# First convolutions of two bottleneck layers on pairs of tiles, with seven half-size products in place of eight

## The chip, the cores and the metric

One core of a Trainium2 chip. The metric is device time in microseconds (us); medians of three or four runs are quoted. Executions of one kernel agree within about 0.2%. Engine names in the profile: PE is the tensor engine (PEld its weight loads), DVE is VectorE, ACT is ScalarE, POOL is GpSimd, SP is SyncE. A bank is one tile of PSUM, the memory that matmuls write and add into. A transfer's landing is the arrival of its data. Half clock is a granted TensorE clock of 0.50 in the profile.

## The reference

Two bottleneck layers in a row, in fp32, on 64 images of 1024 channels and 14 by 14 pixels:

```python
out = relu(bn(conv1x1(x, w1)))        # 1024 -> 256 channels: "first convolution"
out = relu(bn(conv3x3(out, w2)))      # 256 -> 256: "second"
out = bn(conv1x1(out, w3))            # 256 -> 1024: "third"
x   = relu(x + softplus(residual_scale) * out)
```

The batch norm takes mean and variance over the whole batch, so each convolution must be complete before it can be normalised. These are the stage boundaries. The third convolution's statistics come from a "gram" stage of its own, which multiplies the second convolution's output with itself.

## The kernel before

x lies in 32 tiles of two images (128 partitions x 8 channel blocks x 392 pixels). The first convolution is a plain product for each tile and each half of the output channels, eight matmuls into one bank:

```python
def conv1(xt, t, w1, par, stats):
    for o in range(MS):                                   # 2 output halves
        ps = psum_tile()
        for s in range(CS):                               # 8 channel blocks
            nc.tensor.matmul(ps, w1[:, s, o, :], xt[:, s, :], start=(s == 0), stop=(s == CS - 1))   # L136
        y = two(t, o)
        nc.scalar.activation(y, ps..., AF.Identity, bias=...)                                       # L138
        nc.vector.bn_stats(stats[:, o, t, :], y)                                                    # L141
```

In layer 0 ("stage one") this loop runs alone, with x from HBM. In layer 1 it is interleaved with layer 0's third convolution (L305), which makes the tiles that it needs. The 3x3 filters of both layers are transformed on VectorE during stage one. Each of four (layer, input half) pieces is loaded, six results `u` are computed one after the other into two buffers, and each is stored to HBM, from where the second convolution reads it:

```python
for s in range(MS):
    g = pool.tile(...); nc.scalar.dma_start(out=g, in_=w2s[b][:, s])
    ...                                                    # even, quad: 4 instructions
    for i in range(NF):                                    # 6
        u = pool.tile([P, NK, M], FP, tag="us")            # two buffers
        ...                                                # 3 instructions on VectorE
        nc.gpsimd.dma_start(out=us[b][i][:, s], in_=u)     # L130
...
for t in range(T):
    conv1(load_x(xpool, 0, t), t, w1, par[0], stats1)
    if t in (2, 8):
        filters(fpool, t // 8)
```

The kernel's text gives dependencies; the build orders each engine's instructions by its own estimate of when they are ready and needed, unless an instruction is pinned behind the one before it.

## Time and profile before

| | before |
|---|---|
| time | 2309.55 us (2309.44 to 2312.31) |
| TensorE busy | 97% of the span |
| first convolutions | 1024 products, 680.9 us |
| stage one ends (last product) | 349.2 us |
| boundary before the gram stage: first statistics to first normalisation | 697.70 to 705.39, 7.7 us |
| layer 1's first convolution with layer 0's third | 814.8 to 1490.5, 675.7 us |

The prediction below shows the lines and how they are read.

### The profile page before, as it was taken

To read this page: it belongs to the slowest core of one execution; us is meant where nothing else is said; L and a number is where in the kernel's file an instruction comes from. 1 tells how busy PE (TensorE), PEld (TensorE's weight loads), DVE (VectorE), ACT (ScalarE), POOL (GpSimd) and SP (SyncE) were. 2 spreads that over 40 slices of the span, in tenths; PEclk is the share of its full clock that TensorE was granted. 3 is DMA by queue.
4 is the path that set the end of the run, shared out by engine and by line. 5 is a ranking of instruction groups with operands and counts; after the bars stand their busy time and mean duration, and the time that the engine had idled before them with its cause. 6 is when DMAs were issued, how large, how long until landed. Compare 5 with 4: busy or idle time off the path is not lost. (4 is left out here: it accounts for less than half of the span.)

```text
span 2307.8 us, 22580 instructions
## 1 busy us (share of the span) xinstructions
PE 2236.0 (97%) x9264; PEld 1637.6 (71%) x9264; DVE 1077.3 (47%) x1854; ACT 581.4 (25%) x911; POOL 48.4 (2%) x102
## 2 busy tenths in 40 slices
PE   8999997999997999999999999899999899999998
PEld 4555557999997865555555555499999888555554
DVE  3431116878874333223322332377887733444443
ACT  1111115111104023223222322341111040444443
POOL 0100000000000000000000000000000000000000
PEclk9999998999998999999999999999999998999999
DMA  9864424555443033434343432245455420678774
GB/s 358 305 228 157 146 77 179 186 188 200 182 160 148 1 140 140 167 140 164 143 167 140 157 150 112 115 158 194 183 190 195 152 96 22 257 302 310 293 314 174
DMA packets 41863, 409.13 MB, mean 177 GB/s; under 512 B 4640, under 2 KB 4896, under 8 KB 7968
## 3 DMA queue, kind: packets, MB, share of 16 engines
q1 hardware_dynamic: 27936, 282.08, 33.6%
q0 software_dynamic: 12672, 118.49, 12.3%
q10 hardware_dynamic: 1152, 7.12, 0.8%
q8 instruction: 73, 1.20, 0.2%
q14 instruction: 30, 0.25, 0.0%
HBM read 289.18 MB, written 118.49 MB: 177 GB/s over the span
## 5 line engine op out<-in xcount | busy, mean ns | idle before, releaser
L136 PE MATMUL ps<-x,w 128*128 128x392 f32 x2048 | 680.9, 493 | 10.4 <-DMA w<-in_w 10.4
L305 PE MATMUL ps<-y,w 128*128 128x392 f32 x2048 | 686.2, 496 | 0.0
L136 PEld LDWEIGHTS ps<-x,w 128*128 128x128 f32 x2048 | 390.2, 191 | 295.4 <-DMA w<-in_w 10.4
L305 PEld LDWEIGHTS ps<-y,w 128*128 128x128 f32 x2048 | 392.0, 192 | 286.0 <-issue 4.4
L395 DVE SCALAR_TENSOR_TENSOR x<-ps,scale,x 128x392 f32<-128x392 f32 x512 | 320.5, 626 | 335.5 <-PE ps L305 331.7
L396 ACT ACTIVATE x<-x,shift 128x392 f32<-128x392 f32 x512 | 318.3, 622 | 380.6 <-DVE x L395 380.6
L141 DVE BATCH_NORM_STATS2 stats<-y 128x6 f32<-128x392 f32 x128 | 71.6, 567 | 497.9 <-ACT y L138 497.9
L138 ACT ACTIVATE y<-ps,par 128x392 f32<-128x392 f32 x128 | 74.2, 587 | 557.5 <-PE ps L136 516.7
L221 PE MATMUL ps<-sums,u 128*128 128x224 f32 (+1 forms) x768 | 172.1, 347 | 25.2 <-ACT t L161 12.7
L254 DVE TENSOR_TENSOR f<-ps,ms 128x448 f32<-128x448 f32 x192 | 113.4, 602 | 147.0 <-PE ps L234 79.6
L226 PE MATMUL ps<-r,u 128*128 128x224 f32 (+1 forms) x768 | 173.6, 347 | 0.0
L232 PE MATMUL ps<-r,u 128*128 128x224 f32 (+1 forms) x768 | 172.5, 346 | 0.0
L221 PEld LDWEIGHTS ps<-sums,u 128*128 128x128 f32 x768 | 137.4, 190 | 26.6 <-ACT t L161 13.3
L228 PE MATMUL ps<-r,u 128*128 128x192 f32 (+1 forms) x768 | 153.5, 321 | 0.0
L234 PE MATMUL ps<-r,u 128*128 128x192 f32 (+1 forms) x768 | 153.3, 321 | 0.0
L226 PEld LDWEIGHTS ps<-r,u 128*128 128x128 f32 x768 | 141.8, 191 | 1.3
L245 ACT ACTIVATE ms<-ps 128x448 f32<-128x448 f32 (+1 forms) x80 | 41.9, 524 | 390.5 <-PE ps L221 390.5
L232 PEld LDWEIGHTS ps<-r,u 128*128 128x128 f32 x768 | 136.3, 188 | 1.4
L228 PEld LDWEIGHTS ps<-r,u 128*128 128x128 f32 x768 | 132.5, 189 | 1.1
L234 PEld LDWEIGHTS ps<-r,u 128*128 128x128 f32 x768 | 131.9, 188 | 0.9
L336 DVE TENSOR_TENSOR zt<-ps,crow 128x512 f32<-128x512 f32 x98 | 67.8, 693 | 112.1 <-PE ps L334 112.1
L322 PE MATMUL ps<-zt 128*128 128x257 f32 x392 | 119.6, 387 | 0.5 <-DVE zt L336 0.5
(105 smaller groups left out, 1137.1 us busy)
## 6 DMA issues: line engine op xcount, KB each, us to landing
u<-u SPq DMA_DIRECT2D x96, 1280.0 KB, 5.5
x<-in_x SPq DMA_DIRECT2D x64, 1568.0 KB, 6.7
mid<-x POOLq DMA_DIRECT2D x32, 1568.0 KB, 5.4
x<-mid SPq DMA_DIRECT2D x32, 1568.0 KB, 6.6
out<-x POOLq DMA_DIRECT2D x32, 1568.0 KB, 6.3
u<-us POOLq DMA_DIRECT2D x24, 640.0 KB, 7.3
w<-in_w ACTq DMA_DIRECT2D x4, 1152.0 KB, 16.8
w<-in_w ACTq DMA_DIRECT2D x2, 1024.0 KB, 8.7
```

What stands on the lines that cost most here:

```text
L136: nc.tensor.matmul(ps, w1[:, s, o, :], xt[:, s, :], start=(s == 0), stop=(s == CS - 1))
L138: nc.scalar.activation(y, ps.rearrange("p (h l) -> p h l", h=H), AF.Identity, bias=par[:, B1 + o : B1 + o + 1])
L221: nc.tensor.matmul(m[:, o, :n], w(s, D1D2), sums[:, s].rearrange("p l c -> p (l c)"), start=(s == 0), stop=(s == MS - 1),)
L226: nc.tensor.matmul(odd, w(s, D1), r[:, s, :, WH:], start=(s == 0), stop=False)
L228: nc.tensor.matmul(odd[:, :, : WH - 1], w(s, D3), r[:, s, :, WH + 1 :], start=False, stop=(s == MS - 1))
L232: nc.tensor.matmul(even, w(s, D2), r[:, s, :, :WH], start=(s == 0), stop=False)
L234: nc.tensor.matmul(even[:, :, 1:], w(s, D0), r[:, s, :, : WH - 1], start=False, stop=(s == MS - 1))
L254: nc.vector.tensor_tensor(f[:, o].rearrange("p r (i q c) -> p q (r i) c", i=GI, q=2)[:, :, :lines], eos[o][:, :, :n].rearrange("p q (l c) ...
L305: nc.tensor.matmul(ps.rearrange("p (h l) -> p h l", h=H), w3[:, s, o, :], two(t, s), start=(s == 0), stop=(s == MS - 1))
L322: nc.tensor.matmul(g0, zt[:, c, 0:P], zt[:, c, :], start=first, stop=last)
L395: nc.vector.scalar_tensor_tensor(v, ps, scale[:, o : o + 1], v, ALU.mult, ALU.add)
L396: nc.scalar.activation(v, v, AF.Relu, bias=shift[:, o : o + 1])
```

## The change

Intent: a pair of tiles is a product of 2 by 2 blocks (two output halves, two halves of the input channels, two tiles). With Winograd's form of Strassen's method it takes seven half-size products in place of eight, for some sums of inputs, weights and results. A half product is four matmuls. The core of the diff, cut where marked:

```diff
+    def load_w1(pool, b):            # four transfers in place of one
+        w = pool.tile([P, MS, 2, CS // 2, P], FP, tag="w1", ...)
+        for o in range(MS):
+            for h in range(2):
+                nc.scalar.dma_start(out=w[:, o, h], in_=w1s[b][:, o, h])
+    def combine_w1(pool, b, w):      # four sums of weights on VectorE (L113 to L116)
+        nc.vector.tensor_add(s[:, 0], a[1][0], a[1][1])
+        ...
+    def matmul(*args, **kw):         # first and third convolutions: pinned order
+        tc.keep_in_program_order(nc.tensor.matmul(*args, **kw))
     def filters(b):
-            g = pool.tile(...)       # and even, quad, us
+            spare = y_all[:, s, NPX // 2 - GPX :]        # scratch: tail of y from tile 12 on
+            g, even, quad = ...; u = part(15 * M + (i % 2) * NK * M, NK, M)   # two u per input half
-            nc.scalar.dma_start(out=g, in_=w2s[b][:, s])
+            nc.sync.dma_start(out=g, in_=w2s[b][:, s])
+    class Conv1:
+        p1: bu  = A11 X11;  u1 = copy(bu)            (ScalarE)
+        p2: bx  = A12 X21;  y11 = bx + u1            (VectorE)
+        t1: v1 = X12 - X11                           (VectorE, 128 x 1568; L215)
+        t23: v3 = X22 - X12 (L219); v2 = v3 + X11 (L220)
+        p6: bu += S2 v2;    u2 = copy(bu);  v2 = X21 - v2   (L229)
+        p7: bu += S3 v3;    u3 = copy(bu)
+        p5: bp  = S1 v1;    c22: y22 = bp + u3       (VectorE, L198)
+        p4: bu += A22 v2;   y21 = bu
+        p3: bp += S4 X22;   y12 = bp + u2
...
-        for t in range(T):
-            conv1(load_x(xpool, 0, t), t, w1, par[0], stats1)
-            if t in (2, 8):
-                filters(fpool, t // 8)
+        w1 = combine_w1(one, 0, w1)
+        now = start(0); now.p1()
+        for t in range(0, T, 2):
+            now.t23(); now.t1(); now.p2(); now.p6()
+            if t + 2 < T: after = start(t + 2); after.p1()
+            now.p7(); now.p5(); now.c22(); now.p4(); now.p3()
+            now = after
+            if t in (0, 6):
+                filters(t // 6)
...  (layer 1: the same class between the parts of residual(); x buffers 5 -> 4; PSUM pools per stage;
...   w1 = combine_w1(one, b + 1, w1) stands after the third convolution's scale in the text)
```

The class is written here as its formulas (A are the four blocks of w1, S1 to S4 their sums, X the four blocks of the pair).

More of the change, by code (lines that the diff above doesn't have):

```diff
@@ L55 @@
 LINE = GI * W
+BANKS = dict(bu=2, bx=1, bp=1)
 BUFS = dict(u=3, t=3, r=4, sums=4, ms=3, f=2)
@@ L73, in bottlenecks @@
     small = ctx.enter_context(tc.tile_pool(name="small", bufs=2))
-    psum = ctx.enter_context(tc.tile_pool(name="psum", bufs=8, space=bass.MemoryType.PSUM))
     dram = ctx.enter_context(tc.tile_pool(name="dram", bufs=1, space=bass.MemoryType.DRAM))
@@ L87, in two, with psum_pool, load_x @@
         return y_grp[:, s, t // (GI // G), :, j * G * W : (j + 1) * G * W]
-    def load_x(pool, b, t):
+    def psum_pool(bufs=8):
+        return tc.tile_pool(name="psum", bufs=bufs, space=bass.MemoryType.PSUM)
+    def load_x(pool, b, t, parts=1):
         xt = pool.tile([P, CS, PX], FP, tag="x", name=f"x_{b}_{t}")
-        nc.sync.dma_start(out=xt.rearrange("p s f -> p (s f)"), in_=x[t] if b == 0 else mids[t])
+        n = CS // parts
+        for i in range(parts):
+            nc.sync.dma_start(
+                out=xt[:, i * n : (i + 1) * n, :].rearrange("p s f -> p (s f)"),
+                in_=(x[t] if b == 0 else mids[t])[:, i * n * PX : (i + 1) * n * PX],
+            )
         return xt
     def load_w1(pool, b):
-        w = pool.tile([P, CS, MS, P], FP, tag="w1", name=f"w1_{b}")
-        nc.scalar.dma_start(out=w, in_=w1s[b])
-        return w
+        w = pool.tile([P, MS, 2, CS // 2, P], FP, tag="w1", name=f"w1_{b}")
+        for o in range(MS):
+            for h in range(2):
+                nc.scalar.dma_start(out=w[:, o, h], in_=w1s[b][:, o, h])
+        return w
+    def combine_w1(pool, b, w):
+        a = [[w[:, o, h] for h in range(2)] for o in range(MS)]
+        s = pool.tile([P, 4, CS // 2, P], FP, tag="w1s", name=f"w1s_{b}")
+        nc.vector.tensor_add(s[:, 0], a[1][0], a[1][1])
+        nc.vector.tensor_sub(s[:, 1], s[:, 0], a[0][0])
+        nc.vector.tensor_sub(s[:, 2], a[0][0], a[1][0])
+        nc.vector.tensor_sub(s[:, 3], a[0][1], s[:, 1])
+        return a, [s[:, i] for i in range(4)]
     def load_w3(pool, b):
@@ L102, in load_w3, with psum_tile, filters, part @@
         return w
-    def psum_tile(n=PX):
+    def matmul(*args, **kw):
+        tc.keep_in_program_order(nc.tensor.matmul(*args, **kw))
+    def psum_tile(psum, n=PX):
         return psum.tile([P, 512], FP, tag="ps", name="ps")[:, :n]
-    def filters(pool, b):
+    def filters(b):
         for s in range(MS):
-            g = pool.tile([P, 3, 3 * M], FP, tag="w2", name=f"w2_{b}_{s}")
-            nc.scalar.dma_start(out=g, in_=w2s[b][:, s])
-            even = pool.tile([P, 3 * M], FP, tag="even", name="even")
-            quad = pool.tile([P, 3 * M], FP, tag="quad", name="fquad")
+            spare = y_all[:, s, NPX // 2 - GPX :]
+            def part(first, n, m):
+                return spare[:, first : first + n * m].rearrange("p (n m) -> p n m", n=n)
+            g = part(0, 3, 3 * M)
+            even, quad = part(9 * M, 2, 3 * M)[:, 0], part(9 * M, 2, 3 * M)[:, 1]
+            nc.sync.dma_start(out=g, in_=w2s[b][:, s])
             nc.vector.tensor_add(even, g[:, 0], g[:, 2])
@@ L118, in filters @@
             for i in range(NF):
-                u = pool.tile([P, NK, M], FP, tag="us", name="us")
+                u = part(15 * M + (i % 2) * NK * M, NK, M)
                 r = u[:, 0:3, :].rearrange("p k m -> p (k m)")
@@ L130, in filters, with __init__, product, bank @@
                 nc.gpsimd.dma_start(out=us[b][i][:, s], in_=u)
-    def conv1(xt, t, w1, par, stats):
-        for o in range(MS):
-            ps = psum_tile()
-            for s in range(CS):
-                nc.tensor.matmul(ps, w1[:, s, o, :], xt[:, s, :], start=(s == 0), stop=(s == CS - 1))
-            y = two(t, o)
-            nc.scalar.activation(
-                y, ps.rearrange("p (h l) -> p h l", h=H), AF.Identity, bias=par[:, B1 + o : B1 + o + 1]
-            )
-            nc.vector.bn_stats(stats[:, o, t, :], y)
+    class Conv1:
+        def __init__(self, psum, pool, pair, ts, w1, par, stats):
+            self.psum, self.pool, self.ts, self.par, self.stats = psum, pool, ts, par, stats
+            (self.a, self.s), (self.xa, self.xb) = w1, pair
+            self.half = [[t[:, h * CS // 2 : (h + 1) * CS // 2, :] for t in pair] for h in range(2)]
+        def product(self, bank, w, b, first, last):
+            n = CS // 2
+            for i in range(n):
+                matmul(
+                    bank, w[:, i, :], b[:, i, :], start=first and i == 0, stop=last and i == n - 1,
+                    skip_group_check=True,
+                )
+        def bank(self, tag):
+            return self.psum.tile([P, 512], FP, tag=tag, name=tag, bufs=BANKS.get(tag, 1))[:, :PX]
+        def t(self, tag):
+            return self.pool.tile([P, CS // 2, PX], FP, tag=tag, name=tag, bufs=1)
+        def keep(self, bank, tag):
+            v = self.pool.tile([P, PX], FP, tag=tag, name=tag, bufs=1)
+            nc.scalar.activation(v, bank, AF.Copy)
+            return v
+        def result(self, o, i, bank, more=None):
+            t, bias = self.ts[i], self.par[:, B1 + o : B1 + o + 1]
+            y, ps = two(t, o), bank.rearrange("p (h l) -> p h l", h=H)
+            if more is None:
+                nc.scalar.activation(y, ps, AF.Identity, bias=bias)
+            else:
+                nc.vector.scalar_tensor_tensor(
+                    y, ps, bias, more.rearrange("p (h l) -> p h l", h=H), ALU.add, ALU.add
+                )
+            nc.vector.bn_stats(self.stats[:, o, t, :], y)
+        def p1(self):
+            self.bu = self.bank("bu")
+            self.product(self.bu, self.a[0][0], self.half[0][0], True, True)
+            self.u1 = self.keep(self.bu, "u1")
+        def p2(self):
+            b = self.bank("bx")
+            self.product(b, self.a[0][1], self.half[1][0], True, True)
+            self.result(0, 0, b, self.u1)
+        def t1(self):
+            self.v1 = self.t("t1")
+            nc.vector.tensor_sub(self.v1, self.half[0][1], self.half[0][0])
+        def t23(self):
+            self.v3, self.v2 = self.t("t3"), self.t("t2")
+            nc.vector.tensor_sub(self.v3, self.half[1][1], self.half[0][1])
+            nc.vector.tensor_add(self.v2, self.v3, self.half[0][0])
+        def p5(self):
+            self.bp = self.bank("bp")
+            self.product(self.bp, self.s[0], self.v1, True, True)
+        def p6(self):
+            self.product(self.bu, self.s[1], self.v2, False, True)
+            self.u2 = self.keep(self.bu, "u2")
+            nc.vector.tensor_sub(self.v2, self.half[1][0], self.v2)
+        def p7(self):
+            self.product(self.bu, self.s[2], self.v3, False, True)
+            self.u3 = self.keep(self.bu, "u3")
+        def c22(self):
+            self.result(1, 1, self.bp, self.u3)
+        def p4(self):
+            self.product(self.bu, self.a[1][1], self.v2, False, True)
+            self.result(1, 0, self.bu)
+        def p3(self):
+            self.product(self.bp, self.s[3], self.half[1][1], False, True)
+            self.result(0, 1, self.bp, self.u2)
@@ L147, in norm, with conv2 @@
             nc.scalar.activation(y, y, AF.Relu, bias=shift[:, s : s + 1], scale=scale[:, s : s + 1])
-    def conv2(pool, b, par, aff, stats):
+    def conv2(psum, pool, b, par, aff, stats):
         pairs = [(g, p) for g in range(NG) for p in ((1, 2), (3, 4), (0, NF - 1))]
@@ L210, in products @@
                 n = lines * WH
-                m = psum_tile(2 * RT * GI * WH).rearrange("p (o n) -> p o n", o=MS)
+                m = psum_tile(psum, 2 * RT * GI * WH).rearrange("p (o n) -> p o n", o=MS)
                 eos = []
@@ L215, in w @@
                         return u[:, s, k, o * P : (o + 1) * P]
-                    eo = psum_tile(2 * RT * GI * WH).rearrange("p (q n) -> p q n", q=2)
+                    eo = psum_tile(psum, 2 * RT * GI * WH).rearrange("p (q n) -> p q n", q=2)
                     odd, even = (eo[:, q, :n].rearrange("p (l c) -> p l c", c=WH) for q in range(2))
@@ L300, in conv2, with conv3 @@
             acc = finish(g, pair, products(now), acc)
-    def conv3(t, o, w3):
-        ps = psum_tile()
+    def conv3(psum, t, o, w3):
+        ps = psum_tile(psum)
         for s in range(MS):
-            nc.tensor.matmul(
+            matmul(
                 ps.rearrange("p (h l) -> p h l", h=H), w3[:, s, o, :], two(t, s), start=(s == 0), stop=(s == MS - 1)
@@ L308, in conv3, with gram @@
         return ps
-    def gram(pool, aff, crow):
-        g0, g1 = psum_tile(M + 1), psum_tile(P + 1)
+    def gram(psum, pool, aff, crow):
+        g0, g1 = psum_tile(psum, M + 1), psum_tile(psum, P + 1)
         zts = [pool.tile([P, CH, M + 1], FP, tag=f"zt{i}", name=f"zt{i}") for i in range(NZT)]
@@ L329, in gram @@
                 normed += 1
-            tp = psum_tile(CH * M)
+            tp = psum_tile(psum, CH * M)
             for c in range(CH):
@@ L344, in gram, with conv3_stats @@
         return g0, g1
-    def conv3_stats(pool, grams, w3, ccol, mv):
+    def conv3_stats(psum, pool, grams, w3, ccol, mv):
         g0p, g1p = grams
@@ L359, in conv3_stats @@
             nc.vector.tensor_add(m[:, s, 0:1], d, ccol[:, s : s + 1])
-        quad = psum_tile(3 * CS).rearrange("p (o k) -> p o k", k=3)
+        quad = psum_tile(psum, 3 * CS).rearrange("p (o k) -> p o k", k=3)
         ones = keep.tile([P, 1], FP, tag="ones", name="ones")
@@ L366, in conv3_stats @@
             cols = slice(h * half, (h + 1) * half)
-            t0, t1 = psum_tile(half * P), psum_tile(half * P)
+            t0, t1 = psum_tile(psum, half * P), psum_tile(psum, half * P)
             nc.tensor.matmul(t0, g0[:, 0:P], w3[:, 0, cols, :], start=True, stop=True)
@@ L386, in conv3_stats, with residual @@
         nc.vector.tensor_sub(mv[:, :, 1], r[:, :, 2], sq)
-    def residual(pool, b, t, w3, aff):
+    def residual(psum, pool, b, t, w3, aff):
         scale, shift = aff
         xt = load_x(pool, b, t)
+        yield xt
         for o in range(CS):
-            ps = conv3(t, o, w3)
+            ps = conv3(psum, t, o, w3)
             v = xt[:, o, :]
@@ L396, in residual @@
             nc.scalar.activation(v, v, AF.Relu, bias=shift[:, o : o + 1])
-        to = mids[t] if b == 0 else out[t]
-        nc.gpsimd.dma_start(out=to, in_=xt.rearrange("p s f -> p (s f)"))
-        return xt
+            if o == CS - 1:
+                to = mids[t] if b == 0 else out[t]
+                nc.gpsimd.dma_start(out=to, in_=xt.rearrange("p s f -> p (s f)"))
+            yield xt
     def stats_tile(n, name):
@@ L467, in bottlenecks @@
     stats1 = stats_tile(MS, "stats1_0")
-    with tc.tile_pool(name="first", bufs=1) as one, tc.tile_pool(name="first_x", bufs=4) as xpool, tc.tile_pool(
-        name="filters", bufs=2
-    ) as fpool:
+    with tc.tile_pool(name="first", bufs=1) as one, tc.tile_pool(
+        name="first_x", bufs=4
+    ) as xpool, psum_pool() as psum:
         w1 = load_w1(one, 0)
+        pair = [load_x(xpool, 0, t, 2) for t in range(2)]
         for b in range(2):
@@ L476, in bottlenecks, with start @@
         masks.make_identity(nc, ident)
-        for t in range(T):
-            conv1(load_x(xpool, 0, t), t, w1, par[0], stats1)
-            if t in (2, 8):
-                filters(fpool, t // 8)
+        def start(t):
+            xs = pair if t == 0 else [load_x(xpool, 0, t + i) for i in range(2)]
+            return Conv1(psum, one, xs, (t, t + 1), w1, par[0], stats1)
+        w1 = combine_w1(one, 0, w1)
+        now = start(0)
+        now.p1()
+        for t in range(0, T, 2):
+            now.t23()
+            now.t1()
+            now.p2()
+            now.p6()
+            after = None
+            if t + 2 < T:
+                after = start(t + 2)
+                after.p1()
+            now.p7()
+            now.p5()
+            now.c22()
+            now.p4()
+            now.p3()
+            now = after
+            if t in (0, 6):
+                filters(t // 6)
     for b in range(2):
@@ L490, in bottlenecks @@
         stats2 = stats_tile(MS, f"stats2_{b}")
-        with tc.tile_pool(name=f"conv2_{b}", bufs=1) as pool:
-            conv2(pool, b, pb, aff, stats2)
-        with tc.tile_pool(name=f"last_{b}", bufs=1) as one, tc.tile_pool(name=f"last_x_{b}", bufs=5) as xpool:
+        with tc.tile_pool(name=f"conv2_{b}", bufs=1) as pool, psum_pool() as psum:
+            conv2(psum, pool, b, pb, aff, stats2)
+        with tc.tile_pool(name=f"last_{b}", bufs=1) as one, tc.tile_pool(
+            name=f"last_x_{b}", bufs=4 if b == 0 else 5
+        ) as xpool:
             w3 = load_w3(one, b)
@@ L498, in bottlenecks @@
             aff = affine(aggregate(stats2, MS), MS, pb, G2, BE2)
-            grams = gram(one, aff, crow)
-            mv3 = small.tile([P, CS, nc.vector.BN_AGGR_DIM], FP, tag="mv3", name="mv3")
-            conv3_stats(xpool, grams, w3, ccol, mv3)
+            with psum_pool() as psum:
+                with tc.tile_pool(name=f"gram_{b}", bufs=1) as pool:
+                    grams = gram(psum, pool, aff, crow)
+                mv3 = small.tile([P, CS, nc.vector.BN_AGGR_DIM], FP, tag="mv3", name="mv3")
+                conv3_stats(psum, xpool, grams, w3, ccol, mv3)
             aff = affine(mv3, CS, pb, G3, BE3, conv_bias=B3)
@@ L505, in bottlenecks, with run @@
             if b == 1:
-                for t in range(T):
-                    residual(xpool, b, t, w3, aff)
+                with psum_pool() as psum:
+                    for t in range(T):
+                        for _ in residual(psum, xpool, b, t, w3, aff):
+                            pass
                 return
             stats1 = stats_tile(MS, f"stats1_{b + 1}")
-            ahead = residual(xpool, b, 0, w3, aff)
-            for t in range(T):
-                xt, ahead = ahead, residual(xpool, b, t + 1, w3, aff) if t + 1 < T else None
-                conv1(xt, t, w1, par[b + 1], stats1)
+            w1 = combine_w1(one, b + 1, w1)
+            def run(steps, n=None):
+                while n != 0 and next(steps, None) is not None:
+                    n = n and n - 1
+            with psum_pool(4) as psum, tc.tile_pool(name=f"conv1_{b + 1}", bufs=1) as pool:
+                before, rest = None, residual(psum, xpool, b, 0, w3, aff)
+                for t in range(0, T, 2):
+                    xa = next(rest) if t == 0 else xn
+                    run(rest)
+                    if before is not None:
+                        before.p4()
+                        before.p3()
+                    rest = residual(psum, xpool, b, t + 1, w3, aff)
+                    xb = next(rest)
+                    now = Conv1(psum, pool, (xa, xb), (t, t + 1), w1, par[b + 1], stats1)
+                    run(rest, CS // 2)
+                    now.t1()
+                    run(rest)
+                    now.p1()
+                    now.p2()
+                    now.p5()
+                    now.t23()
+                    now.p6()
+                    if t + 2 < T:
+                        rest = residual(psum, xpool, b, t + 2, w3, aff)
+                        xn = next(rest)
+                        run(rest, 1)
+                    now.p7()
+                    now.c22()
+                    before = now
+                before.p4()
+                before.p3()
 def kernel(**inputs):
@@ L530, in packed @@
         w1 = get("w1").reshape(P, MS, P, CS).transpose(2, 3, 1, 0)
+        w1 = w1.reshape(P, 2, CS // 2, MS, P).transpose(0, 3, 1, 2, 4)
         w2 = get("w2").reshape(P, MS, P, MS, 3, 3).transpose(2, 3, 4, 5, 1, 0).reshape(P, MS, 3, 3 * M)
```

## The prediction

> **What bounds the kernel now.** I read the page's busy shares first, then the costliest groups, then who waited for whom on the tensor engine, then busy time by stage.
>
> ```profile
> PE 2236.0 (97%) x9264; PEld 1637.6 (71%) x9264; DVE 1077.3 (47%) x1854; ACT 581.4 (25%) x911; POOL 48.4 (2%) x102
> ...
> L136 PE MATMUL ps<-x,w 128*128 128x392 f32 x2048 | 680.9, 493 | 10.4 <-DMA w<-in_w 10.4
> L305 PE MATMUL ps<-y,w 128*128 128x392 f32 x2048 | 686.2, 496 | 0.0
> ```
>
> TensorE is busy for 97% of the span, and the first convolutions (L136) take 680.9 us of it. Each fp32 product has two records, so 2048 records are 1024 products: 680.9/1024 = 0.665 us each. The column's mean of 493 ns overlaps its neighbour and is not the pitch. The busy share alone would not prove a full engine, since ends are modelled; the waits do.
>
> ```profile
> PE ps L334 <- ACT y L147: 23.6, 4, 11.0
> PE ps L221 <- ACT t L161: 12.7, 1, 12.7
> PE ps L221 <- DVE sums L201: 12.5, 1, 12.5
> PE ps L136 <- DMA w<-in_w: 10.4, 1, 10.4
> ```
>
> Columns: total us, times, longest. The waits sit at four stage boundaries and at the start; inside a convolution there are none. So removed matmul time should come off one for one, unless a new wait appears. By stage (us, then busy us of PE, PEld, DVE, ACT, POOL, clock, DMA share, GB/s):
>
> ```profile
> 10.40:349.20 338.80, 338.77 (x1024) 195.40 (x1024) 83.60 (x178) 37.87 (x68) 13.34 (x24) 1.00 0.57 207
> 806.00:1491.00 685.00, 684.52 (x2084) 398.11 (x2084) 199.59 (x338) 196.69 (x321) 17.01 (x32) 0.99 0.36 141
> 0.00:57.70 57.70, 47.31 (x140) 27.29 (x141) 20.16 (x61) 6.24 (x12) 4.76 (x13) 1.00 0.93 358
> 57.70:115.40 57.70, 57.70 (x177) 33.38 (x176) 24.57 (x47) 7.08 (x13) 5.86 (x12) 1.00 0.85 305
> ```
>
> The first row is layer 0's first convolution, the second is layer 1's, which is interleaved with layer 0's third. VectorE is used for 25% and 29% there: room for the new additions on average. The last two rows are the filter preparation in the first stage, where DMA is at 93% and 85%. There VectorE waits for filter buffers (start, us, engine, line, what, idle before):
>
> ```profile
> 46.25 0.42 DVE L129 TENSOR_TENSOR us<-us 128x256 f32<-128x256 f32 x1
> 55.54 0.56 DVE L122 TENSOR_SCALAR us<-w 128x768 f32<-128x768 f32 x1 [8.87 <-DMA u<-us]
> ...
> 140.57 5.71 DVE L141 BATCH_NORM_STATS2 stats<-y 128x6 f32<-128x392 f32 x12
> ```
>
> A filter instruction held VectorE's queue for 8.87 us, and twelve statistics instructions piled up behind such waits until 140.57. It cost nothing, because no matmul needed those statistics. After the change matmuls will need VectorE.
>
> **What the Trainium skill says.** "VectorE: DVE Perf Modes", section "Why `tensor_tensor` can't do 2×_2P or 4×": a sum of two tensors needs both read ports, so fp32 gets one result per cycle. The trace agrees: 448 elements take 0.620 us and 896 take 1.084, a slope of (1.084-0.620)/448 = 1.036 ns per element. "TensorE: Matmul & The Clock Gate", section "Architectural detail: the array is 16× 32×32, not 1× 128×128": VectorE and ScalarE are strict FIFO; the pile of twelve above agrees. Same page, section "The HAM clock gate (the "warmup" mystery)": after about 3.4 us of idleness the matmul clock falls to half. Here the first four matmuls after a wait of 12.68 us took 1.83 us, where later groups of four take 0.92; so a long new gap costs about 2 us more than its length and a short one doesn't. "PSUM — Partial Sum Buffer", section "The four PSUM rules": a matmul without the start flag adds to what the bank holds, and a partial sum may be read in the middle. The new chain of sums depends on it; no run shows it yet, because before every bank is finished before it is read.
>
> **The change, part by part.** A convolution of a pair of x tiles is a 2 by 2 block product (two output halves, two input-channel halves, two tiles), done with seven half products in place of eight. A half product is 4 matmuls.
>
> 1. *Matmuls removed.* A pair falls from 32 products to 28. In stage one: 338.77/512 = 0.662 us each, 64 fewer, 42.3 us. In layer 1: 21.06 us per 32 products (in order of time, one tile's start at 1448.22 and the next work's at 1458.76, 10.54 us per 16), 0.659 us each, 64 fewer, 42.1 us. Together 84.4 us.
>
> 2. *VectorE added.* Per pair four sums of 128x1568: 1.084 + 672 x 0.001036 = 1.78 us each, 7.1 us (an estimate from the slope). Three results are added from PSUM by VectorE at 0.63 us (the row of L395 has that form), 1.9 us; four statistics at 0.57 us stay, 2.3 us. In all 11.3 us of a pair's 28 x 0.66 = 18.5 us. In layer 1 there are 16 residual additions besides, 10.0 us: 21.3 of 21.1 + 18.5 = 39.6 us. It fits both, so it lies beside the matmuls. ScalarE gets three copies of about 0.59 us (duration of L138) and loses three results: no change.
>
> 3. *New waits in steady state.* Three sums share a bank: a product must wait until the sum before it has been copied out, about 0.2 us to see the end plus 0.59 plus a signal, 0.9 us. In stage one a half product of the next pair (2.63 us) lies between, or P5 does; in layer 1 one third-convolution output (1.32 us) does. Both cover 0.9. The tightest: P3 adds to P5's bank, which VectorE must have read during P4's 2.63 us; it needs 0.2 + 0.63 + 0.1 and may find a 1.78 us sum ahead of it, 2.7 us, so up to 0.1 lost. The second-factor sum of the next pair can start only when P4 has read the buffer, and is needed 5.26 us later. Nothing lost. Layer 1's last pair lacks the filler: 0.9 twice, 2 us. Stage one's last pair, 1 us.
>
> 4. *Start.* The first half product needs only a quarter of w1 and half of x0, so it starts earlier than 10.4 us. But the third product needs both tiles, 3.2 MB plus 1 MB of weights and parameters: at 321 GB/s in the first 10.4 us (busy time by stage) and up to 430 after it (the view of the DMA queues), about 13 us, then two sums of 1.78 us, so 17 us. Two products of 2.63 us are done by then: the effective start is 17 - 5.3 = 11.7, and the gap is long enough for a half clock again, 2 us. Loss 3 us.
>
> 5. *Filters in y's spare part.* The same 24 filter tiles, but both input halves have buffers of their own and may overlap. By pitch of the rows, VectorE needs about 11.1 us for each of four halves, 44 us. They must be gone by the time the seventh pair writes there. Six pairs are 6 x 18.5 = 111 us after a start at 12; the demand is 44 + 6 x 11.3 = 112 us. So VectorE is nearly full for six pairs, and its queue holds waits of up to 9 us on DMA landings, while slack before a matmul starves is 2 to 5 us. I take 8 us lost, an allowance between none (everything interleaves) and 25 (each of a dozen waits costs two).
>
> 6. *Pinned order, four x buffers in layer 1, w1 in four transfers.* An x load takes 6.6 us to land and its buffer comes free a pair (39 us) ahead: nothing. The stage before third convolution had them filling PSUM during 3.2 us of scale computation (814.76 to 817.95); four banks hold 5.3 us, so nothing is lost.
>
> Sum: 84.4 - 2 - 1 - 3 - 8 = 70.4, so 2309.55 - 70.4 = 2239 us, a factor of 1.031.
>
> **The rivals.** (a) *VectorE becomes the bound while filters are made.* For it: term 5's balance without reserve and waits in a strict queue. Against: the transfers' DMA share in stage one is 0.57 on average, and filter work is pieces of at most 0.96 us. It would cost 15 to 30 us: 2246 to 2261. (b) *Short waits in every pair*, from the shared banks and the pinned order, since no other matmul may fill a gap. One us per pair is 32 us: 2263. Against: each chain of term 3 has a filler. (c) *Everything overlaps*, also the start: 84.4 less 3, 2228. (d) *Loads bound stage one.* A pair needs 3.2 MB in 18.5 us, 174 GB/s, and once the filters are done (150 to 340 us) the stage ran at a DMA share of 0.38; so not beyond the first 100 us.
>
> **Range and chances.** Best case (c) with a little more at the start gives 2226; (a) in full gives 2260. Range 2226 to 2260. Two per cent is 46 us, or 2263; that takes (a) and (b) at once, or a layer 1 that doesn't gain. Faster by over 2%: 0.89; within: 0.10; slower: 0.01.
>
> **What would show it.** Matmul records at stage-one shape fall from 2048 to 1792, with unchanged pitch; layer 1's stage shortens by 40 us without waits inside; stage one by some 30, with its lost time in the first 130 us as waits of PE on VectorE sums and of VectorE on filter landings. After the seventh pair a pair takes 18.5 us. Wrong would be: a regular wait in each pair (rival b), a stage boundary grown by more than 3 us, or waits on x loads in layer 1.

## The result, and the profile after

2289.6 us (2287.83 to 2290.83, four runs) against 2310.39 for before in the same rounds: ratio 0.9908, 95% interval 0.9891 to 0.9926. A ratio is the mean time of one kernel's runs over that of the other's runs in the same rounds, so it is not quite the ratio of the medians. The output is correct. The change gained 21 us where 70 were predicted, which lies outside the range; the prediction had given 0.89 to more than 2% faster, and this is within 2%.

First the page of the changed kernel: busy shares and the groups that answer to L136 and L305 (all pinned matmuls now have the helper's line L126, so the tiles tell them apart).

```profile
PE 2164.1 (95%) x9008; PEld 1592.5 (70%) x9008; DVE 1357.5 (59%) x2086; ACT 571.0 (25%) x911; POOL 48.3 (2%) x102
...
L126 PE MATMUL ps<-y,w 128*128 128x392 f32 x2048 | 686.7, 495 | 0.6 <-DVE quad L485 0.3
...
L126 PE MATMUL bu<-t,w1s 128*128 128x392 f32 x512 | 187.1, 510 | 29.4 <-DVE t L220 28.1
```

The engine has 9264 - 9008 = 256 records fewer, as predicted. But its busy share fell too: the time is in new idleness, named in the last column. Who the tensor engine waited for (total us, times, longest):

```profile
PE ps L437 <- ACT y L250: 39.1, 4, 26.4
PE bu L126 <- DVE t L220: 28.1, 3, 12.2
PE bp L126 <- DVE y L198: 7.4, 2, 5.7
PE bu L126 <- DMA w<-in_w: 7.0, 1, 7.0
PE bu L126 <- ACT u L189: 1.9, 3, 0.6
```

Two things grew: waits inside stage one for VectorE's sums (L220, L198), and the wait at the gram stage (before: 23.6 in total, 11.0 the longest; now 39.1 and 26.4). By stretch, in the columns that the prediction explains:

```profile
7.04:150.00 142.96, 107.49 (x284) 59.76 (x285) 105.28 (x173) 12.76 (x26) 13.17 (x24) 0.86 0.77 288
150.00:352.60 202.60, 201.93 (x613) 116.01 (x611) 117.81 (x121) 23.64 (x44) 0.00 (x0) 1.00 0.42 151
703.00:727.00 24.00, 0.14 (x1) 0.17 (x2) 8.40 (x22) 2.18 (x3) 0.00 (x0) 0.53 0.73 287
833.40:1469.60 636.20, 634.80 (x1920) 365.49 (x1920) 336.39 (x450) 189.79 (x321) 17.00 (x32) 1.00 0.40 154
```

| | before | after | predicted after |
|---|---|---|---|
| stage one ends | 349.2 | 352.6 | 319 |
| boundary before the gram stage | 7.7 | 23.1 (701.89 to 725.02) | 7.7 |
| layer 1's stretch | 675.7 | 636.1 (833.46 to 1469.6) | 635.6 |

Layer 1 gained its 40 us to within a microsecond. Stage one gained nothing: after 150 us it runs nearly without a wait (201.93 of 202.60 us busy), but before that the tensor engine was busy for only 107.49 of 142.96 us. And one boundary, where no matmul was changed, lost 15 us.

The boundary, in order of time (start, us, engine, line, what, in brackets the idle time before and its releaser), first its two ends in the kernel before, then the changed kernel:

```profile
697.70 3.84 DVE L289 BATCH_NORM_STATS2 stats<-y 128x6 f32<-128x392 f32 x8
...
705.39 20.72 ACT L147 ACTIVATE y<-y,shift,scale 128x1568 f32<-128x1568 f32 x13 [1.61 <-DVE shift L435]
```

```profile
705.65 1.89 DVE L512 BATCH_NORM_AGGREGATE mv<-stats 128x2 f32<-128x192 f32 x2
717.84 0.69 DVE L115 TENSOR_TENSOR w1s<-w 128x512 f32<-128x512 f32 x1 [10.31 <-DMA w<-in_w]
718.45 0.16 DVE L523 TENSOR_SCALAR v<-mv 128x2 f32<-128x2 f32 x1
...
721.79 0.69 DVE L113 TENSOR_TENSOR w1s<-w 128x512 f32<-128x512 f32 x1 [3.10 <-DMA w<-in_w]
...
725.02 20.72 ACT L250 ACTIVATE y<-y,shift,scale 128x1568 f32<-128x1568 f32 x13 [6.17 <-DVE shift L540]
```

The scale of the second convolution (L523 and on) was ready to be computed at 707.5. In VectorE's queue the build had put sums of layer 1's weights ahead of it and between it. They are first needed about 140 us later (861.90), but they waited for w1 to land, 10.31 and 3.10 us, and everything behind them waited too.

Stage one, the first and the last of its bad places, tensor engine and VectorE:

```profile
41.50 2.80 PE L126 MATMUL bx<-x,w 128*128 128x392 f32 x8
56.51 5.59 PE L126 MATMUL bu<-t,w1s 128*128 128x392 f32 x8 [12.21 <-DVE t L220]
```

```profile
47.39 0.95 DVE L156 SCALAR_TENSOR_TENSOR y<-y 128x768 f32<-128x768 f32 x1
48.26 1.79 DVE L219 TENSOR_TENSOR t<-x 128x1568 f32<-128x1568 f32 x1
50.44 0.96 DVE L156 SCALAR_TENSOR_TENSOR y<-y 128x768 f32<-128x768 f32 x1 [0.39 <-DMA u<-y]
...
54.67 1.79 DVE L220 TENSOR_TENSOR t<-t,x 128x1568 f32<-128x1568 f32 x1
...
126.11 0.96 DVE L156 SCALAR_TENSOR_TENSOR y<-y 128x768 f32<-128x768 f32 x1 [6.42 <-DMA u<-y]
...
131.35 1.78 DVE L220 TENSOR_TENSOR t<-t,x 128x1568 f32<-128x1568 f32 x1
```

At 41 to 56 us VectorE is busy nearly without a gap: filter work (the rows of y<-y) stands in front of and between the two sums, and the product that needs L220 starts 12.21 us late. From 119.7 to 131 us it is mostly idle, yet the sum comes late too: a filter instruction at the head of the queue waits 6.42 us for a store to land and free its buffer. The half clock after such a wait costs more: the product after the wait of 12.21 us took 5.59 us in place of 2.80.

So there are two candidates within stage one, work in front and waits for landings, both by way of the strict queue. The rivals: the sheer volume of VectorE work, and late transfers.

### The profile page after: what moved, and what is told of

Same layout as the page of the kernel before. It is cut to its first block, busy times and chain, and to the rows that moved or that the text cites. A ratio compares the mean times of both kernels' runs of the same rounds, so it can differ in the third digit from the quotient of the medians.

```text
span 2286.1 us, 22406 instructions
## 1 busy us (share of the span) xinstructions
PE 2164.1 (95%) x9008; PEld 1592.5 (70%) x9008; DVE 1357.5 (59%) x2086; ACT 571.0 (25%) x911; POOL 48.3 (2%) x102
## 4 chain that ended last, share of the span: by engine, by line
PE 90%; issue 4%; DVE 2%; DMA 2%; ACT 1%; POOL 0%; ACTq 0%; POOLq 0%
PE ps L126 29%; PE bu L126 14%; PE bp L126 7%; PE ps L329 6%; PE ps L324 6%; PE ps L335 6%; PE ps L331 5%; PE ps L337 5%; PE ps L425 4%; PE bx L126 3%; PE ps L426 2%; PE ps L437 2%; DMA w<-in_w 1%; DMA u<-y 1%; PE ps L483 1%
## 5 line engine op out<-in xcount | busy, mean ns | idle before, releaser
L126 PE MATMUL ps<-y,w 128*128 128x392 f32 x2048 | 686.7, 495 | 0.6 <-DVE quad L485 0.3
L126 PEld LDWEIGHTS ps<-y,w 128*128 128x128 f32 x2048 | 391.1, 191 | 287.7 <-issue 4.4
L126 PE MATMUL bu<-t,w1s 128*128 128x392 f32 x512 | 187.1, 510 | 29.4 <-DVE t L220 28.1
L126 PEld LDWEIGHTS bu<-t,w1s 128*128 128x128 f32 x512 | 100.1, 197 | 105.5 <-DVE t L220 21.4
L189 ACT ACTIVATE u<-bu 128x392 f32<-128x392 f32 x96 | 47.7, 497 | 385.2 <-PE bu L126 385.2
L229 DVE TENSOR_TENSOR t<-x,t 128x1568 f32<-128x1568 f32 x32 | 57.3, 1792 | 84.2 <-PE bu L126 84.2
```

The costliest lines, as they stand in the source:

```text
L126: tc.keep_in_program_order(nc.tensor.matmul(*args, **kw))
L229: nc.vector.tensor_sub(self.v2, self.half[1][0], self.v2)
```

## The experiments

Ten kernels, each timed in three rounds beside the kernel before, whose median was 2310.4 to 2310.9 us every time, so times of different sessions are compared directly. "Changed" is the kernel of the diff; times are medians.

**1. Layer 1's weight sums behind the scale** (changed, with one pin):

```diff
-        nc.vector.tensor_add(s[:, 0], a[1][0], a[1][1])        # and the three after it
+        pin(nc.vector.tensor_add(s[:, 0], a[1][0], a[1][1]))
-            w1 = combine_w1(one, b + 1, w1)
+            w1 = combine_w1(one, b + 1, w1, tc.keep_in_program_order)
```

> Only change: layer 1's four weight sums are kept behind the scale computation on VectorE. Theory A (strict queue): the changed kernel's wait before the gram stage grew by 15.4 us (from 7.7 us between first statistics of the second convolution and the first normalisation to 23.1 us) because these sums stood in VectorE's queue, waiting 10.3 and 3.1 us for w1, ahead of the scale. Then the gap falls back to about 7.7 us and the time by 15 us, to about 2274 us; first stage unchanged. Rival (w1 and x transfers themselves, or the four issues on ScalarE's queue, delay the stage): under 3 us gained, and the wait reappears elsewhere.

Measured: 2274.48 us, ratio to before 0.9844, correct. That is 15.1 us less than the changed kernel, and the gap is 7.7 us again:

```profile
702.43 3.84 DVE L392 BATCH_NORM_STATS2 stats<-y 128x6 f32<-128x392 f32 x8
...
710.13 25.47 ACT L250 ACTIVATE y<-y,shift,scale 128x1568 f32<-128x1568 f32 x16 [1.61 <-DVE shift L540]
```

The w1 transfers are as they were; only what stood behind them in the queue was set free. The boundary is settled.

**2. Filter transfers without filter arithmetic** (changed; wrong result):

```diff
-            nc.vector.tensor_add(even, g[:, 0], g[:, 2])       # and all filter arithmetic
             for i in range(NF):
-                nc.gpsimd.dma_start(out=us[b][i][:, s], in_=u)
+                nc.gpsimd.dma_start(out=us[b][i][:, s], in_=part(0, NK, M))
```

> Filter transfers as before (four loads, 24 stores of the same size) but without any filter arithmetic on VectorE; result wrong on purpose. Theory A (VectorE's queue holds the convolution's sums up behind filter work): the four waits of the first stage after its start (12.2, 5.7, 1.7, 7.9 us and the half clock after them, about 35 us in all) vanish, the first stage ends near 318 us in place of 352.6, time about 2254 us. Rival (transfers: x or the shared DMA engines are late): at least half of the waits stay, time above 2270 us.

Measured: 2260.14 us, 29.5 less than the changed kernel; 35 had been expected. Three of the four waits are gone. One stayed, and it is of another kind:

```profile
78.86 1.79 DVE L204 TENSOR_TENSOR t<-x 128x1568 f32<-128x1568 f32 x1 [13.28 <-DMA x<-in_x]
80.57 0.62 DVE L183 SCALAR_TENSOR_TENSOR y<-bp,par,u 128x392 f32<-128x392 f32 x1
...
81.24 5.60 PE L126 MATMUL bp<-x,w1s 128*128 128x392 f32 x8 [6.96 <-DVE y L183]
```

A sum of the next pair waited for its x at the head of the queue, with a result behind it that could have run. That x tile was late by this experiment's own doing: stores now read the filter tile itself, so the second layer's load of it waits for them, and the x loads stand behind that load in SyncE's queue. In the changed kernel neither VectorE nor the tensor engine ever waits for x after the start of stage one, so late x explains none of its waits; but the mechanism is the same.

**3. Filter arithmetic and transfers, without the landing waits** (changed; wrong result):

```diff
-                nc.gpsimd.dma_start(out=us[b][i][:, s], in_=u)
+                nc.gpsimd.dma_start(out=us[b][i][:, s], in_=part(0, NK, M))
```

> Filter arithmetic and transfers both stay, but the stores read another place, so no filter instruction waits for a store to land; result wrong on purpose; the scheduler may order VectorE anew. Theory A1 (waits for landings inside the queue are the larger part): the waits of 5.7, 1.7 and 7.9 us go, the one of 12.2 (VectorE busy without a gap) stays: about 20 us gained, 2270 us. Rival V (sheer volume of VectorE work): the waits stay about as large in sum, under 8 us gained.

Measured: 2270.55 us, 19 less, which is the expected number, but partly by luck. The three waits went, as expected. One wait is left in stage one after the start:

```profile
61.69 4.29 PE L126 MATMUL bu<-t,w1s 128*128 128x392 f32 x8 [18.15 <-DVE t L220]
```

But the wait of 12.2 us, which was to stay, grew to 18.15: the build, free of the buffers, put still more filter work ahead of the second pair's sums. The order changed with the dependency, so this run doesn't separate the two candidates cleanly. The next ones fix the order.

**4. Filter work spread over nine pairs, VectorE's order pinned** (changed, with run 1's pin). All VectorE instructions of stage one are pinned; the filter work becomes 32 parts, one or two in each of three gaps of a pair; the two input halves take turns; scratch is moved to the last 19 x 256 columns of y, so that it may be used until the tenth pair; `even` and `quad` get tiles of their own. The core of the edit, without the conditions for the first parts:

```diff
+            now.p2(); some(k, 1); now.c11()
+            now.p6(); some(k, 1); now.t2b()
+            ...; after.p1(); now.p7(); some(k, 2); after.t3()
+            now.p5(); now.c22(); after.t1(); now.p4m(); after.t2(); now.c21(); now.p3m(); now.c12()
-            nc.sync.dma_start(out=g, in_=w2s[b][:, s])
+            nc.gpsimd.dma_start(out=gs[s], in_=w2s[b][:, s])
```

> Right result. The same filter arithmetic, stores and buffer count, but all VectorE work of the first stage in a fixed order with the filter work cut in 32 pieces and given to gaps of nine pairs (filters placed later in y), two rows of the filters alternating so that a buffer comes round once per pair; plus the late weight sums of the first run. Theory A (order and waits in the queue, not volume): no wait over 2 us in the first stage after its start, stage ends at 318 to 323 us, and with the 15 us of the boundary about 2242 us. Rival V (volume): VectorE can't hold it and the first stage still loses over 15 us, time above 2258 us.

Measured: 2249.06 us, ratio 0.9733, correct. After its start stage one has no wait above 1 us, with the same arithmetic and stores, so their volume by itself is no bound. (Over nine pairs, that is; whether six would hold it isn't tested. The changed kernel doesn't suggest that VectorE was full there: it was busy for 105.28 of the 142.96 us before 150 us.) The missing 7 us are in the start, where one thing went wrong:

```profile
35.29 5.56 PE L126 MATMUL bu<-t,w1s 128*128 128x392 f32 x8 [19.79 <-DVE t L242]
```

My filter loads were issued at 1.3 us on GpSimd's queue, ahead of half of what the start needs.

**5. The same with the filter loads on SyncE's queue, behind the first x loads:**

```diff
-            nc.gpsimd.dma_start(out=gs[s], in_=w2s[b][:, s])
+            nc.sync.dma_start(out=gs[s], in_=w2s[b][:, s])
```

> The spread kernel again, but its four filter loads go through SyncE's queue behind the first x loads, as in the changed kernel. The spread kernel's only wait in the first stage (19.8 us before the first third product) came with its filter loads issued at 1.3 us on GpSimd's queue, w1 landing at 18 to 21 us and the parameters at 25 to 29 us. Theory A (start lost to these loads): the third product starts at 20 to 23 us in place of 35.3, 12 to 15 us gained, about 2236 us, no other wait over 2 us. Rival (the fixed VectorE order itself delays the start): start stays above 30 us, time above 2245 us.

Measured: 2233.92 us, ratio 0.9666 (0.9651 to 0.9680), correct. The third product starts at 20.39 us in place of 35.29, and this stretch of the stage has neither waits nor a lower clock:

```profile
60.00:140.00 80.00, 80.00 (x244) 46.17 (x243) 67.91 (x88) 9.31 (x18) 5.84 (x11) 1.00 0.81 298
```

VectorE is 85% busy there and DMA 81%, and the tensor engine never waits. So the order itself doesn't delay the start, and the loads did. In the changed kernel the same 80 us held 64.70 us of tensor work and 59.07 of VectorE work.

**6. A changed start on top of it:** softplus moved to the eleventh pair, and the first pair's fifth product, which needs half of x1, ahead of its sixth.

```diff
+        now.p1(); now.p2(); some(0, 1); now.t1(); now.p5(); now.t3(); now.t2()
+            if t == 20:
+                sps = [softplus(p, b) for b, p in enumerate(par)]
```

> The kernel of the run before plus a changed start: the softplus chain moved to the eleventh pair and the first pair's fifth product (needs only half of x1) put ahead of its sixth. Theory: the start is bound by the landing of x1 and then two sums of 1.79 us; one product of 2.63 us moves into that wait and the sums stand behind no parameter: 3 to 6 us less than the run before, about 2232 us. Rival (landing alone decides): under 2 us.

Measured: 2232.33 us, ratio 0.9661, correct: 1.6 us less than run 5, and the intervals of the two overlap. Both beat the changed kernel and the one before. The expectation of 3 to 6 us was missed: the sixth product moved up only to 19.19 us with one more product done before it, and then the next pair's first product met its own x still in flight:

```profile
24.74 4.59 PE L126 MATMUL bu<-x,w 128*128 128x392 f32 x8 [2.68 <-DMA x<-in_x]
```

**7. Run 5 with the filter work of each layer in one piece:**

```diff
-            some(k, 1); ... some(k, 1); ... some(k, 2)      # in each pair's gaps
+            if t in (0, 12):
+                some(k, 16)
```

> As the run with later loads, same instructions and buffers, VectorE order fixed, but the filter work of each layer stands in one piece of 16 parts (about 22 us of VectorE work plus waits for landings) between two pairs. Theory A (what stands ahead of the convolution's sums in the strict queue decides): two waits of 15 to 25 us each in the first stage, time 2268 to 2290 us. Rival V (volume of VectorE work decides, place doesn't): time within 5 us of that run.

Measured: 2270.11 us, 36 more than run 5. VectorE had no wait for a landing at all in this run; the two blocks of filter work, each 24 us long, were enough:

```profile
PE bu L126 <- DVE t L253: 30.8, 2, 15.4
```

Each block costs 15.4 us of waiting and a product at half clock (5.53 and 5.57 us). Work in front of the sums is shown as a cause by itself.

**8. One sum moved in the changed kernel's first pair**, so that the two sums that the sixth product needs come ahead of the one for the fifth:

```diff
-            now.t1()
+            now.t1(tc.keep_in_program_order if t == 0 else lambda ins: ins)
```

> The changed kernel with one sum moved: in the first pair the sum for the fifth product comes after the two sums that the sixth needs (in the changed kernel it ran first, 16.32 to 18.1 us). If that order cost the start, the wait of 7.96 us falls by 1.8 us and the time to about 2288; if the landing of x1's second half (about 18.5 us) decides, nothing changes (2289.6).

Measured: 2286.05 us, 3.5 less than the changed kernel, but the intervals of the two ratios overlap (0.9878 to 0.9907, and 0.9891 to 0.9926). What is shown is the start, by one trace of each. The third product in the changed kernel, then in this one:

```profile
22.73 5.57 PE L126 MATMUL bu<-t,w1s 128*128 128x392 f32 x8 [7.96 <-DVE t L220]
```

```profile
20.79 5.18 PE L126 MATMUL bu<-t,w1s 128*128 128x392 f32 x8 [5.86 <-DVE t L220]
```

The order cost the start 2 us, as the first theory said. The rest of the gain I don't ascribe, since this kernel's own times (2283.89 to 2288.28) scatter by more.

**9. Run 5 with the halves one after the other**, so that a buffer comes round after two parts:

```diff
-        for i in range(NF):
-            for s in range(MS):
+        for s in range(MS):
+            for i in range(NF):
```

> The kernel of the run with later loads, same instructions, buffers and slots in the fixed VectorE order, but the filters' two input halves are worked one after the other (as in the changed kernel's text) in place of by turns, so a filter buffer comes round after two parts in place of four, 5 to 10 us in place of 18; a store takes 7 us to land (median). Theory A1 (a filter instruction that waits for a landing holds up the convolution's sums behind it): VectorE waits for landings appear in the first stage, 2 to 5 us each, part of them starve the tensor engine, 5 to 20 us slower than that run (2239 to 2254 us). Rival (slack absorbs the landings; only the amount of work in front counts): within 3 us of it.

Measured: 2234.42 us, no different from run 5. I had expected waits of 2 to 5 us; there were four, and the longest was 1.9 us. A miss of size, and a useful one: waits that short cost nothing here.

**10. The same with one buffer per half:**

```diff
-                u = bufs[s][i % 2]
+                u = bufs[s][0]
```

> The kernel of the run before (halves in turn) with one filter buffer per half in place of two, so each part waits for the part before it to land (6.1 us median there); same amount of VectorE work and same order. That run's waits of at most 1.9 us cost nothing. Theory A1 (a wait for a landing at the head of the strict queue starves the tensor engine once it is longer than the slack of 1.4 to 6 us): waits of 3 to 7 us in each of eight pairs, 15 to 45 us slower, 2249 to 2279 us, the tensor engine waiting on VectorE sums or results. Rival (only work in front counts, waits for landings don't): within 3 us of 2234.

Measured: 2283.53 us, 49 more than run 9, a little beyond the expected range. Who waited for whom in it, VectorE first:

```profile
DVE y L166 <- DMA u<-y: 46.5, 12, 5.8
DVE y L163 <- DMA u<-y: 12.5, 3, 4.6
```

```profile
PE bp L126 <- DVE y L210: 39.6, 6, 9.6
```

Arithmetic and order are those of run 9. Fifteen waits for landings of up to 5.8 us (59 us in sum) turned into 40 us of waiting on the tensor engine, and half clock after it. Before the wait of 9.6 us at 64.08, for instance, two waits for landings (2.33 and 4.51 us) stood ahead of one result. So waits for landings are shown as a cause by themselves as well, once they exceed what the pair can absorb.

## Why the prediction was wrong, point by point

- *Matmuls removed* (84.4 us). Right: 256 records fewer, and an undisturbed half product starts 2.633 us after the one before, so 128 x 0.658 = 84.3 us. (In what follows a loss is the spacing of the starts of products less 2.633.)
- *VectorE's cost and steady waits* (parts 2 and 3). Right: the sums took 1.785 to 1.792 us on average (1.78 estimated), and in layer 1 and after 150 us in stage one no bank or buffer holds a product up. The last pairs waited three times 0.6 us and lost 2.7 us in all; 3 had been taken. The correct output is the first run of this case that shows partial sums read in the middle of a sum.
- *Start* (3 us). Wrong in size: 8.5. The third product started at 22.73 us, not 17, so the effective start is 17.5 us, 7.1 later than before; the half clock after the wait cost 3.0, not 2, and 1.5 comes off because the kernel before began at half clock too. Before that product VectorE ran the softplus chain until 16.3 us and then a sum that wasn't urgent. From run 8, 2 us of it is order. The landing was taken too early as well: in run 6, with the softplus moved away, the sum that needs all of x1 still waited for x until 15.43 us, where the prediction had 13.
- *Filters* ("I take 8 us lost"). This is the main step that failed: the size put on an overlap that wasn't there. The four waits are 12.2 + 5.7 + 1.7 + 7.9 = 27.5 us by the profile and 28.2 by spacing, and the half clock after them 8.0, so 36. The prediction had the parts: a strict queue, waits of up to 9 us at its head, VectorE nearly full until the scratch is overwritten. It then took an even interleaving and a small allowance. But the order in the queue is set at build time, before any landing is known (and it isn't the text's order, which has each layer's filter work in one block between two pairs): it put more than 10 us of filter work ahead of sums that a product was due to need, and waits for landings ahead of others. Rival (a) placed the loss rightly, in VectorE's queue while filters are made, though what held the sums up was order and waits rather than a full engine. The upper end of its range, 30 us, was nearly the size; it was treated as the unlikely case.
- *Volume.* The balance "44 + 6 x 11.3 = 112 of 111 us" was sound arithmetic, but it isn't what cost the time: run 5 does the same work over nine pairs beside the matmuls without a wait, and in the changed kernel VectorE was busy for 74% of the stretch before 150 us. Whether six pairs could hold it is untested.
- *w1 in four transfers, buffers, pools: "nothing"* (part 6). Wrong: 15.4 us, the second step that failed. One of the prediction's own signs of being wrong, a boundary grown by more than 3 us, came true here. I looked at what x, PSUM and transfers would do and not at the four new weight sums, which part 2 doesn't list either; they had no urgency and could stand anywhere in VectorE's queue. Run 1 shows that their place alone made the loss.
- *Layer 1* (40.1 us gained net). Right: 39.6.

Together: -84.3 + 8.5 + 36 + 2.7 + 15.4 = -21.7, and the two profiled runs differ by 21.7 (2309.54 and 2287.83 us). With order repaired (run 5) the kernel takes 2233.9 us; the prediction without its 8 us for the filters gives 2231. So its matmul arithmetic held, and what failed was the assumption about where VectorE's work would stand. What stays open is how the 36 us divide between work in front and landings in the changed kernel itself: runs 7 and 10 show both causes, each in an order of my own. The changed kernel's trace suggests work in front for the wait of 12.2 us, and landings for those of 5.7 and 7.9 (VectorE stood 5.09 and 6.42 us for a store just before them), but no run tests that division alone.

## What to carry to other kernels

When an engine with slack joins the critical path, its busy share says little: ask what stands ahead of each urgent instruction in its strict queue, and what the head of that queue may wait for. Pin urgent instructions, cut other work on that engine into pieces smaller than the slack, and give its buffers a round trip longer than a transfer takes to land. Preparatory work for a later stage wants a pin too, since the build may place it in front of a stage boundary, as in run 1's boundary here.

## What the Trainium skill lacked or had wrong

- "TensorE: Matmul & The Clock Gate", section "Architectural detail: the array is 16× 32×32, not 1× 128×128", says that VectorE is strict FIFO, but neither there nor in the pages I read is it said what a blocked head costs when a build orders the queue: here four small weight sums cost 15.1 us (run 1), waits of up to 1.9 us cost nothing (run 9), and waits of up to 5.8 us cost 49 us (run 10).
- The same page, section "The HAM clock gate (the "warmup" mystery)", gives an idle window of about 3.4 us before the half clock. After waits of 5.68, 7.91 and 12.21 us the trace agrees (products of 5.12 to 5.59 us in place of 2.80), but in run 6 a wait of 2.68 us, with two gaps under 1 us in the 10 us before it, was followed by a product of 4.59 us, with a mean granted clock of 0.55 from 25.6 to 28.8 us. That is one execution, and waits of up to 1.72 us were followed by products of 2.90 us; but the window's length isn't a safe limit.
